# A four-part residual block on one core: the diagonal mix moved within its period, an epsilon added on another engine, and eight weight sums placed in other slots

## Chip, core and metric

One core of a Trainium2 chip runs the whole program. The metric is the time of one execution in device microseconds, the median of several runs. Engines are named as in the profile: PE (TensorE) with PEld for its weight loads, DVE (VectorE), ACT (ScalarE), POOL (GpSimd), SP (SyncE, which here only starts transfers). "L435" is line 435 of the kernel before.

## What is computed

`x` is 64 x 32 x 512 in float32. Four blocks follow each other, each adding its result to `x`; cut to what matters here:

```python
def block0(x, condition, weights):            # W is 32x32 for each of 64 samples
    return einsum('bct,bcd->bdt', x, weights[condition])

def block1(x, adapter_ids, base_weight, base_bias, A_w, B_w):
    result = einsum('bsd,od->bso', x, base_weight) + base_bias
    h = einsum('bsd,brd->bsr', x, A_w[adapter_ids])       # rank 16
    return result + einsum('bsr,bor->bso', h, B_w[adapter_ids])

def block2(x, Wq, Wk, Wv, Wo, q_norm_w, k_norm_w, k_cache, v_cache, table, seqlens):
    q, k, v = heads(x @ Wq.T), heads(x @ Wk.T), heads(x @ Wv.T)   # 32 / 8 / 8 heads of 128
    q, k = rope(rmsnorm(q, q_norm_w)), rope(rmsnorm(k, k_norm_w))
    # rmsnorm: t * rsqrt(mean(t*t) + EPS) * w
    keys, values = paged_cache(k_cache, table) + k, paged_cache(v_cache, table) + v  # 512 + 32
    probs = softmax(where(valid, q @ keys.T / sqrt(128), -1e30))
    return (probs @ values) @ Wo.T

x = x + block0(...); x = x + block1(...); x = x + block2(...)
x = x + block3(...)                            # as block0, other weights
```

The change touches block 0 (the mix), the rmsnorm of block 2, and the preparation of block 2's projection weights.

## The kernel before

**Tiles.** The 2048 rows of `x` form 16 tiles of 128 rows, each holding four samples. Block 0 is one matmul for a tile: four 32 x 32 matrices are spread into a 128 x 128 block-diagonal matrix (`diagonal`, L426: the gathered rows `mix_rows` times a mask `same`), multiplied with the tile (`mix`, L435), and added to it on DVE (`add`, L444). Block 1 needs the tile transposed (`turn_x`, L452), the low-rank product `h` (`ranks`, L474), its mask (`own_ranks`, L484, DVE), and a linear product in five chunks (`linear`, L490): four of the base weight, the fifth with the masked ranks `hT`. GpSimd adds the bias (L447). The result is turned again (`turn_out`) and stored for block 2. Tiles are taken in pairs; each second tile also makes sums and differences of the pair's transposed halves (`sums`, L516 to 520), because the projections are done with seven products instead of eight, from sums of inputs and sums of weights.

**Projections.** Eight key heads are done in two groups of four. In each group, eight pairs of tiles are projected; a pair has three blocks of seven products each: keys and values, and two for the queries. `project` (L651) issues two matmuls for each product into `proj_ps`, which is one PSUM bank, and `take` (L663, DVE; ACT for the first of a block) adds it to what was kept. Products 1, 4, 5, 6 of a queries' block, and two of the keys' and values' block, start a `Norm`: `squares` (L707, four ACT instructions with a running sum), `power` (L712 adds epsilon on DVE, L714 raises to the power -1/2 on GpSimd), and then four pieces `scale`, `straight`, `swapped`, `sum` on DVE, and a turn on PE. `swapped` and `straight` read the rotary tiles `rot_q` and `rot_k`, which SP loads for each pair (`load_rotary`, L591).

**Weight sums.** `block_sum` (L615, DVE, 1.14 us each) makes the sums of weights for a group: four for keys and values (`KV`), four each for query blocks 0 and 1. The query sums are made in the first pair's window of a group.

**Attention.** 512 units of work, one for each sample and key head, follow each other: scores against 544 keys (L838, L841), a masked maximum and softmax (L846, L857, L863), a transposition of the weights (L880, L882), and the product with the values (L893), whose rows GpSimd gathers (`v_sb`, L105). GpSimd also makes the penalty mask of a sample (`pen`, L809), 2.23 us each. The last phase, from about 2112 us, multiplies with `Wo` and adds block 3.

**Order.** Every engine works its queue in the order in which the program was written, and that is set by a hand-made plan: time is cut into slots, an attention slot lasting about 3.66 us. `at(slot, where, ...)` puts a step into a list of a slot, and `slot(i)` issues the lists one after the other:

```python
run(i, "fetch"); run(i, "pool")      # transfers
...                                   # scores of this unit, flip of an earlier one
run(i, "pe"); run(i, "late"); run(i, "power")
norm_piece(i)
... ; run(i, "turn") ; ...            # values, divide
run(i, "dve")
norm_piece(i); norm_piece(i)
run(i, "keep"); run(i, "act"); run(i, "store")
```

Norm pieces wait in a queue of their own, and a slot takes one only while its count `busy[slot]` is under 2 (3 in every fourth slot); a `block_sum` puts 2 on the count of its slot.

The slots before attention form the prologue (0 to about 240 us). There a tile `t` has a home slot -39 + 2t, so that a period is two slots. In the first slot of the period of tile t, PE does the mix of t, projections of an earlier pair, the ranks and linear chunks 0 to 2 of t-1, and the turn of t-2. In the second it does linear chunks 3 and 4 of t-1, projections, and the turn of t. On DVE the first slot has `own_ranks` of t-1 and the add of the mix of t, ahead of its "dve" list (takes, `block_sum`); the second has the add of the linear result of t-1 and then its "dve" list: `sums`, the diagonal of t+1, rotary tiles (L382), takes. The cache's key pages are turned as well, four of them in the first slots (class `Turn`).

Of the kernel before, what the change touches and what calls it, by code (L numbers as in the profile page):

```python
# [30 lines left out]
ALU = mybir.AluOpType  # L31
# [17 lines left out]
D = 128  # L49
# [10 lines left out]
EPS = 1e-6  # L60
# [17 lines left out]
def resid_kernel(  # L78
# [19 lines left out]
    nc = tc.nc  # L98
# [129 lines left out]
    with ExitStack() as l2:  # L228
# [468 lines left out]
        class Norm:  # L697
# [11 lines left out]
                    )  # L709

            def power(self):
                nc.vector.tensor_scalar(self.ss, self.ss, D * EPS, None, ALU.add)  # L712
                self.rstd = small.tile([P, REP], F32, name="rstd")
                nc.gpsimd.tensor_tensor(  # L714
                    self.rstd, self.ss, minus_half.to_broadcast([P, REP]), ALU.pow
                )
# [220 lines left out]
        def at(slot, where, do, *args):  # L937
            plan.setdefault((slot, where), []).append((do, args))
# [56 lines left out]
        def make(table, key, what, *args, **kw):  # L995
            table[key] = what(*args, **kw)
# [5 lines left out]
        for i in range(n_pairs):  # L1002
            home = WINDOW * (i - 1) - AHEAD
            g, p = divmod(i, NT // 2)
            if i == 0:
                at(home - 10, "fetch", make, pair_of, 0, Pair, 0)
            for w, name in ((23, "a"), (26, "12"), (29, "34"), (30, "b")):
                if i + 1 < n_pairs:
                    if name == "a":
                        at(home + w, "store", make, pair_of, i + 1, Pair, i + 1)  # L1010
                    at(home + w, "store", call, pair_of, i + 1, "load", name)
            if i == 0:
                at(home + 4, "store", call, pair_of, 0, "load", "b")
            if i:
                at(home + 2, "fetch", call, pair_of, i, "load_rotary", "k")
                at(home + 9, "fetch", call, pair_of, i, "load_rotary", "q")
            for b, slots in (
                (KV, (0, 0, 1, 2, 3, 3, 4, 5, 6, 6, 7, 8, 9, 9)),
                (0, (10, 11, 12, 12, 13, 14, 15, 15, 16, 17, 18, 18, 19, 20)),
                (1, (21, 21, 22, 23, 24, 24, 25, 26, 27, 27, 28, 29, 30, 30)),  # L1020
            ):
                slots = [home + w for w in slots]
                at(slots[0], "fetch", begin_block, i, b, slots)
            if p == 0:
                sums = [(b, what) for b in (0, 1) for what in (3, 2, 1)] + [(0, 4), (1, 4)]
                for w, one in zip((5, 6, 7, 9, 10, 11, 17, 18), sums):
                    at(home + w, "dve", block_sum, *one)
                    busy[home + w] = busy.get(home + w, 0) + 2
                for w, what in zip((-1, 0, 2, 5) if g == 0 else (-19, -16, -13, -10), (3, 2, 1, 4)):
                    at(home + w, "dve", block_sum, KV, what)  # L1030
                    busy[home + w] = busy.get(home + w, 0) + 2
            if p == NT // 2 - 1:

                if g == NG - 1:
                    loads = [(load_o_weights, k) for k in range(2 * KG)]
                else:
                    loads = [(load_kv_weights, g + 1, k) for k in (1, 0)]
                    loads += [(load_q_weights, g + 1, k) for k in range(KG)]
                if g == NG - 1:
                    places = (  # L1040
                        (7, 8), (11, 12), (16, 18), (20, 21), (23, 25), (36, 38), (27, 29), (24, 26)
                    )
                else:
                    places = ((3, 4), (9, 10), (14, 15), (21, 22), (25, 26), (32, 33))
                for slots, load in zip(places, loads):
                    for j, w in enumerate(slots):
                        at(home + w, "store", *load, j, nc.gpsimd)
# [4 lines left out]
        for t in range(NT):  # L1052
            home = -WINDOW - AHEAD - 6 + 2 * t
            f = [first_of, t]
            at(home - 5 if t > 1 else begin, "fetch", make, *f, First, t)
            at(home - 4 if t > 1 else begin, "fetch", call, *f, "load")
            at(max(begin, home - 4) if t > 1 else begin, "pool", call, *f, "fetch")
            if t % 2 == 0:
                at(home - 3 if t else begin, "pool", call, *f, "fetch_a")
            at(home - 2, "dve", call, *f, "diagonal")  # L1060
            at(home - 1, "pe", call, *f, "mix")
            at(home - 1, "power", call, *f, "add")
            if t % 2 == 0:
                at(home, "turn", call, *f, "turn_a")
                at(home, "keep", call, *f, "keep_a")
            at(home, "turn", call, *f, "turn_x")
            at(home, "keep", call, *f, "keep_x")
            at(home + 1, "pool", call, *f, "bias")
            at(home + 1, "late", call, *f, "ranks")
            at(home + 1, "power", call, *f, "own_ranks")  # L1070
            at(home + 1, "late", call, *f, "linear", (0, 1, 2))
            at(home + 2, "pe", call, *f, "linear", (3, 4))
            at(home + 2, "power", call, *f, "add")
            at(home + 3, "store", call, *f, "store_x")
            at(home + 3, "turn", call, *f, "turn_out")
            at(home + 3, "keep", call, *f, "keep_out")
            at(home + 4, "store", call, *f, "store")
            if t % 2:
                at(home + 4, "dve", call, *f, "sums")
                at(home + 5, "store", call, *f, "store_sums")  # L1080

            home = SLOTS * t + 9
            turning.add(home)
            at(home - 6, "fetch", lambda t: make(turn_of, t, Turn, 1, t, room["pages"], 1), t)
            at(home, "turn", call, turn_of, t, "turn")
            at(home, "keep", call, turn_of, t, "keep")
            at(home + 1, "store", call, turn_of, t, "store")
        for c in range(NT):


            home = -27 + c if c > 3 else begin + 3 + c
            key = -1 - c
            at(home - 3 if c > 3 else begin, "fetch", make, turn_of, key, Turn, 0, c, start_pool, 5)
            where = "turn" if c > 3 else "pe"
            at(home, where, call, turn_of, key, "turn")
            if 0 < c < 4:
                plan[home, where].insert(0, plan[home, where].pop())
            at(home, "keep", call, turn_of, key, "keep")
            at(home + 1, "store", call, turn_of, key, "store")
            home = -27 + max(c - 1, 0) * 10 // NT  # L1100
            at(home, "dve", rotary, c)
            at(home, "store", store_rotary, c)
# [54 lines left out]
        home = n - 33  # L1157
# [132 lines left out]
    with ExitStack() as l3:  # L1290
        sums = l3.enter_context(tc.tile_pool(name="sums", bufs=1))
# [196 lines left out]
```

## Time and profile before

| | us |
|---|---|
| median of three runs | 2515.36 |
| the three runs | 2513.62, 2515.36, 2519.85 |
| the profiled execution | 2515.45 |
| its span | 2513.7 |
| PE busy | 2454.2 (13760 instructions) |
| DVE busy | 1626.6 (3762) |
| ACT busy | 1398.6 (4135) |
| POOL busy | 1124.8 (936) |

The span is what the profile divides; some 1.7 us of the execution lie around it. A row of a group of instructions gives line, engine, operation, output and inputs, the number of instructions, their busy time and mean duration, and how long the engine was idle just ahead of them and for whom. A row of the waits reads "engine, what it was about to do, whom it waited for: total us, times, longest". A row of the timeline has start and duration in us; consecutive instructions of one kind are one row with a count, and the bracket at the end is the idle time before it and its releaser. A releaser ending in "q" or an engine ending in "q" is the engine's queue of transfers.

### The profile page before, as it was taken

To read this page: it belongs to the slowest core of one execution; us is meant where nothing else is said; L and a number is where in the kernel's file an instruction comes from. 1 tells how busy PE (TensorE), PEld (TensorE's weight loads), DVE (VectorE), ACT (ScalarE), POOL (GpSimd) and SP (SyncE) were. 2 spreads that over 40 slices of the span, in tenths; PEclk is the share of its full clock that TensorE was granted. 3 is DMA by queue.
4 is the path that set the end of the run, shared out by engine and by line. 5 is a ranking of instruction groups with operands and counts; after the bars stand their busy time and mean duration, and the time that the engine had idled before them with its cause. 6 is when DMAs were issued, how large, how long until landed. Compare 5 with 4: busy or idle time off the path is not lost.

```text
span 2513.7 us, 47403 instructions
## 1 busy us (share of the span) xinstructions
PE 2454.2 (98%) x13760; PEld 1863.4 (74%) x13760; DVE 1626.6 (65%) x3762; ACT 1398.6 (56%) x4135; POOL 1124.8 (45%) x936
## 2 busy tenths in 40 slices
PE   6888999999999999999999999999999999999999
PEld 3445777777777777767777777777777788888887
DVE  5656777777777677767776777777777766433222
ACT  2124777777777676757676777777677765000000
POOL 4334555555555555645455555555555663000000
PEclk9999999999999999999999999999999999999999
DMA  7675666666666667756565656565657784333221
GB/s 234 220 236 168 186 198 188 197 194 197 183 203 184 197 192 246 238 179 187 176 186 172 202 173 190 176 187 177 186 173 222 248 257 149 126 124 127 86 84 60
DMA packets 448546, 459.19 MB, mean 183 GB/s; under 512 B 51424, under 2 KB 379488, under 8 KB 440480
## 3 DMA queue, kind: packets, MB, share of 16 engines
q1 hardware_dynamic: 398384, 291.24, 37.4%
q0 software_dynamic: 49904, 164.93, 21.8%
q8 instruction: 112, 1.84, 0.3%
q14 instruction: 146, 1.20, 0.2%
HBM read 384.66 MB, written 79.69 MB: 185 GB/s over the span
## 4 chain that ended last, share of the span: by engine, by line
PE 92%; DVE 2%; DMA 2%; issue 2%; SPq 1%; POOL 0%; ACT 0%; DVEq 0%; ACTq 0%
PE proj_ps L651 22%; PE o_ps L893 17%; PE out_ps L1312 15%; PE s_ps L838 10%; PE s_ps L841 8%; PE pT_ps L880 8%; PE head_ps L756 3%; PE l_ps L490 2%; PE o_ps L905 2%; DMA kT<-kT 1%; SPq L794 1%; PE h_ps L474 1%; PE mix_ps L435 1%; PE s_ps L873 1%; PE mix_ps L1330 1%
## 5 line engine op out<-in xcount | busy, mean ns | idle before, releaser
L105 POOL DMA_INDIRECT v_sb<-v,v_rows x512 | 525.1, 1026 | 359.6 <-PE o_ps L893 248.3
L846 DVE CUSTOM_DVE_ANT_0 sm<-s_ps,pen 128x544 f32<-128x544 f32 x512 | 370.6, 724 | 462.8 <-PE s_ps L841 445.9
L893 PEld LDWEIGHTS o_ps<-pT,v_sb 128*128 128x128 f32 x4096 | 519.8, 192 | 133.1 <-issue 125.0
L857 ACT ACTIVATE sm<-sm,top 128x544 f32<-128x544 f32 x512 | 382.0, 746 | 344.1 <-DVE top L846 343.7
L893 PE MATMUL o_ps<-pT,v_sb 128*128 128x128 f32 x4096 | 541.7, 275 | 1.5 <-DMA v_sb<-v,v_rows 1.5
L863 ACT ACTIVATE sm<-sm,share 128x512 f32<-128x512 f32 x512 | 369.9, 722 | 174.6 <-DVE share L862 169.0
L714 POOL TENSOR_TENSOR rstd<-ss,minus_half 128x4 f32<-128x4 f32 x160 | 208.1, 1301 | 527.5 <-DVE ss L712 527.4
L882 DVE COPY pT<-pT_ps 128x512 f32<-128x512 f32 x512 | 350.9, 685 | 1.9 <-PE pT_ps L880 1.9
L838 PE MATMUL s_ps<-kT,qT 128*128 128x288 f32 x1024 | 347.6, 421 | 3.5 <-DMA kT<-kT 3.3
L841 PE MATMUL s_ps<-kT,qT 128*128 128x256 f32 x1024 | 305.6, 380 | 3.7 <-DMA kT<-kT 3.7
L880 PE MATMUL pT_ps<-ident,sm 128*128 128x128 f32 x2048 | 308.0, 273 | 0.0
L880 PEld LDWEIGHTS pT_ps<-ident,sm 128*128 128x128 f32 x2048 | 256.3, 141 | 51.6 <-issue 0.2
L809 POOL TENSOR_SCALAR pen<-key_f,seq_f 128x544 f32<-128x544 f32 x128 | 285.5, 2231 | 10.8
L841 PEld LDWEIGHTS s_ps<-kT,qT 128*128 128x128 f32 x1024 | 194.6, 190 | 59.2 <-issue 4.3
L663 DVE TENSOR_TENSOR raw<-proj_ps,raw 128x512 f32<-128x512 f32 x332 | 223.1, 684 | 10.2 <-PE proj_ps L651 4.7
L707 ACT ACTIVATE sq<-raw 128x128 f32<-128x128 f32 x640 | 197.1, 308 | 33.3 <-DVE raw L663 18.1
L651 PE MATMUL proj_ps<-sum,x 128*128 128x512 f32 x380 | 189.6, 602 | 2.7 <-DVE raw L663 2.6
L1362 ACT COPY p<-out_ps 128x256 f32<-128x256 f32 x7 | 2.6, 372 | 333.1 <-PE out_ps L1312 298.1
L105 POOL DMA_INDIRECT mix_rows<-in_w,cond_rows x32 | 33.1, 1034 | 312.9 <-DVE mix_diag L171 300.0
L838 PEld LDWEIGHTS s_ps<-kT,qT 128*128 128x128 f32 x1024 | 155.1, 191 | 20.3 <-issue 4.0
L1312 PE MATMUL out_ps<-w,o_in 128*128 128x256 f32 x768 | 167.1, 379 | 0.0
L1312 PEld LDWEIGHTS out_ps<-w,o_in 128*128 128x128 f32 x768 | 145.9, 190 | 19.8
(175 smaller groups left out, 3391.1 us busy)
## 6 DMA issues: line engine op xcount, KB each, us to landing
kT<-kT SPq DMA_DIRECT2D x2048, 64.0 KB
o<-oT SPq DMA_DIRECT2D x29, 1024.0 KB
o_in<-o SPq DMA_DIRECT2D x28, 1024.0 KB
page_rows<-in_kv_cache SPq DMA_DIRECT2D x32, 256.0 KB
v<-in_kv_cache SPq DMA_DIRECT2D x32, 256.0 KB
kT<-page_rows SPq DMA_DIRECT2D x32, 256.0 KB
vn<-raw SPq DMA_DIRECT2D x32, 256.0 KB
v_sb<-v,v_rows POOLq DMA_INDIRECT x512, 4.1
```

Of the source, the lines that this page charges most:

```text
L105: nc.gpsimd.indirect_dma_start(out=dst, out_offset=None, in_=table, in_offset=bass.IndirectOffsetOnAxis(ap=index, axis=0),)
L651: nc.tensor.matmul(self.ps, lhsT=self.pair.x[x][:, c if x == "b" else half.start + c, :], rhs=blocks(self.b)[w][:, c, :], start=(c == 0), ...
L809: nc.gpsimd.tensor_scalar(self.pen, key_f, seq_f[:, self.b : self.b + 1], BIG, ALU.is_ge, ALU.mult)
L838: nc.tensor.matmul(ps[:, first:HID], lhsT=q, rhs=self.kT[:, :n1, k, :], start=True, stop=True)
L841: nc.tensor.matmul(ps[:, HID : first + LA], lhsT=q, rhs=self.kT[:, n1:, k, :], start=True, stop=True)
L846: nc.vector.tensor_tensor_reduce(out=sm, in0=ps[:, first : first + LA], in1=self.pen, scale=1.0, scalar=3e38, op0=ALU.add, op1=ALU.min, ac ...
L857: nc.scalar.activation(sm, sm, AF.Exp, bias=top, scale=-1.0, accum_out=total)
L863: nc.scalar.activation(sm[:, :L], sm[:, :L], AF.Copy, scale=share)
L880: nc.tensor.transpose(ps[:, c, :], self.sm[k][:, c * P : (c + 1) * P], ident)
L882: nc.vector.tensor_copy(pT, ps)
L893: nc.tensor.matmul(self.o_ps[k], lhsT=self.v[c][:, k * D : (k + 1) * D], rhs=self.pT[k][:, c, :], start=(c == 0), stop=False,)
L1312: nc.tensor.matmul(ps[:, :HALF], lhsT=o[:, i, :], rhs=w[i // REP][:, i % REP, :], start=(i == 0), stop=(i == KG * REP - 1),)
```

## The change

Three edits, all to the plan or to the engine that an operation runs on.

1. The diagonal of a tile is made in the list "power" of its slot instead of "dve", that is directly after the add of the linear result; the mix is issued from the list "late" instead of "pe", that is after the ranks and linear chunks 0 to 2 of the tile before. The first page's turn goes to "late" with it.
2. The epsilon in `Norm.power` is added by GpSimd instead of DVE.
3. The eight query sums of a group's first pair go to other slots, in another order: from offsets 5, 6, 7, 9, 10, 11, 17, 18 to 5, 7, 10, 13, 15, 17, 20, 23.

```diff
             def power(self):
-                nc.vector.tensor_scalar(self.ss, self.ss, D * EPS, None, ALU.add)
+                nc.gpsimd.tensor_scalar(self.ss, self.ss, D * EPS, None, ALU.add)
                 self.rstd = small.tile([P, REP], F32, name="rstd")
                 nc.gpsimd.tensor_tensor(
                     self.rstd, self.ss, minus_half.to_broadcast([P, REP]), ALU.pow
                 )
...
             if p == 0:
-                sums = [(b, what) for b in (0, 1) for what in (3, 2, 1)] + [(0, 4), (1, 4)]
-                for w, one in zip((5, 6, 7, 9, 10, 11, 17, 18), sums):
-                    at(home + w, "dve", block_sum, *one)
+                for w, b, what in (
+                    (5, 0, 3),
+                    (7, 0, 2),
+                    (10, 0, 1),
+                    (13, 1, 3),
+                    (15, 1, 2),
+                    (17, 0, 4),
+                    (20, 1, 1),
+                    (23, 1, 4),
+                ):
+                    at(home + w, "dve", block_sum, b, what)
                     busy[home + w] = busy.get(home + w, 0) + 2
...
-            at(home - 2, "dve", call, *f, "diagonal")
-            at(home - 1, "pe", call, *f, "mix")
+            at(home - 2, "power", call, *f, "diagonal")
+            at(home - 1, "late", call, *f, "mix")
             at(home - 1, "power", call, *f, "add")
...
-            where = "turn" if c > 3 else "pe"
+            where = "turn" if c > 3 else "pe" if c else "late"
             at(home, where, call, turn_of, key, "turn")
```

No instruction is added or removed in all: 160 of them go from DVE to GpSimd, and the rest change places. The order in which SP starts its transfers is the same.

## The prediction

> **What bounds the kernel now.** I read the page first: busy shares, the slices, the shares of the chain.
>
> ```profile
> PE 2454.2 (98%) x13760; PEld 1863.4 (74%) x13760; DVE 1626.6 (65%) x3762; ACT 1398.6 (56%) x4135; POOL 1124.8 (45%) x936
> ...
> PE   6888999999999999999999999999999999999999
> ...
> PE 92%; DVE 2%; DMA 2%; issue 2%; SPq 1%; POOL 0%; ACT 0%; DVEq 0%; ACTq 0%
> ```
>
> TensorE is busy nearly everywhere and carries 92% of the chain. Its count of matmuls stays, so the change can win only where PE idles or is clocked down: the first four slices of 63 us. The second view is busy time by stretch (PE, PEld, DVE, ACT, POOL, then the granted clock, DMA share, GB/s).
>
> ```profile
> 28.10:57.10 29.00, 24.61 (x83) 13.61 (x84) 21.84 (x39) 5.66 (x8) 10.18 (x8) 0.88 0.58 189
> 57.10:98.00 40.90, 34.23 (x122) 18.31 (x121) 23.69 (x54) 7.64 (x18) 12.74 (x11) 0.96 0.65 209
> 98.00:139.00 41.00, 33.41 (x119) 18.11 (x118) 26.29 (x70) 9.66 (x28) 13.15 (x10) 0.92 0.76 242
> 139.00:180.00 41.00, 35.77 (x150) 21.26 (x148) 23.11 (x47) 12.48 (x34) 15.59 (x13) 0.96 0.78 240
> 180.00:211.00 31.00, 30.09 (x110) 16.56 (x111) 16.28 (x32) 8.48 (x26) 8.52 (x10) 0.94 0.39 126
> 211.00:241.00 30.00, 23.37 (x84) 13.59 (x83) 22.37 (x52) 17.14 (x50) 18.19 (x17) 0.89 0.68 208
> 300.00:900.00 600.00, 600.00 (x3603) 452.13 (x3602) 431.26 (x1055) 429.57 (x1288) 316.80 (x251) 1.00 0.66 195
> 1104.00:1118.00 14.00, 10.65 (x44) 7.57 (x43) 5.51 (x13) 5.99 (x18) 4.46 (x5) 0.76 0.64 181
> ```
>
> In steady attention PE has 600 of 600 us. In the prologue's periods (28 to 211) it idles 4.39+6.67+7.59+5.23+0.91 = 24.8 us, at the hand-over to attention (211 to 241) 6.6, at the switch between groups of heads (1104 to 1118) 3.35. Third, who is waited for, and one prologue period on the timeline:
>
> ```profile
> PE mix_ps L435 <- DVE mix_diag L426: 28.8, 11, 8.8
> PE proj_ps L651 <- DVE raw L663: 11.9, 7, 5.3
> ...
> POOL rstd L714 <- DVE ss L712: 527.4, 158, 8.9
> ```
>
> ```profile
> 97.75 0.60 PE L452 MATMUL x1T_ps<-ident,x_sb 128*128 128x128 f32 x4
> 100.64 1.13 PE L435 MATMUL mix_ps<-x_sb,mix_diag 128*128 128x512 f32 x2 [2.29 <-DVE mix_diag L426]
> ```
>
> Within 28 to 211 the diagonal costs PE 20.0 us over ten waits, the one proj bank 5.4 over three. In the period shown PE stands 2.29 us at the mix because DVE makes the diagonal (at 100.31) only after four L516-520 sums.
>
> [...] after 5.28 us of idling for `raw` at 222.96, four passes of projections took 3.78 us, where two at 216.65 took 1.02; after 4.16 us of idling at 49.02 the mix took 2.07 us instead of the 1.13 below. [...] at 98.56 one L519 sum took 1.49 us beside a bias add, its neighbours 0.41 to 0.42. [...] The pow of 1.40 us at 337.14 is followed by a gather at 338.73: 1.6 us by starts, so the rows serve.
>
> **Part 1: mix to the period's end, diagonal to its front.** Per tile PE's order was: mix, projections, ranks h, linear 0-2 | linear 3-4, projections, turns; the bar separates the two slots. Now the mix stands before the bar. One matmul (two passes, 0.86 us) moves behind h (0.89) and linear 0-2 (2.58), so it ends about 3.4 us later relative to them; the first page turn (four transposes, 0.44) moves in the same slot. The diagonal (one DVE operation, 0.28) moves ahead of sums, rotary and take. SP's order and the gathers of mix_rows on POOL stay. No instruction is added.
> Removed: the 20.0 us of waits at L435 in the periods. The other 8.8 are the program's first wait, for a gather of mix_rows that lands at 8.49; they stay.
> Added: DVE's add L444 keeps its place (hT, add, then its list) and now waits for the late mix. Queued behind it are the sums, rotary tiles and L663 takes, and the next projection waits for the take, since proj has one bank. Worked for one period with the sums (tiles at slots -26/-25): after the mix, hop 0.27, add 0.60, list 1.14+1.62; then add-linear and diagonal 0.80; then sums 1.46, rotary 0.81, take 1.20, and 1.07 for the collision with the bias add; hop back 0.13. From its second slot on that makes 9.1 us against 3.5 of PE work: 5.6 us of stall. By the same sum the periods come to 1.6, 2.3, 0, 4.1, 5.6, 1.6, 4.4, 2.9, 0, 0.6, 3.3, 0, 0.4 = 26.8 us, against 24.8 + 1.6 (one mix at the edge) = 26.4 before. Clock: (1-PEclk) times length was 11.9 us; I estimate 10.6 from the new stall lengths. So the large wait is replaced by the bank's wait, nearly even: **-1 us**, bounds -10 (DVE slips under the matmuls oftener than I sum) and +10 [...].
>
> **Part 2: epsilon on GpSimd.** 160 operations of L712 (0.16 us each, 26 us) leave DVE; POOL gets 160. In steady state PE has no idle time, so DVE's 26 us are worth nothing; they hid under 600/600 us of PE. POOL's eps now waits for ACT's squares, and behind it stand the pow L714 (1.30), penalty masks (2.23) and v_sb gathers. POOL reaches pow already waiting (527.4 us at L712), so the wait changes owner. The price of a 128x4 constant add on POOL isn't shown. Bounds 0.1 (the 128x1 memset is 0.09) and 1.3 (pow, same shape); I take 0.35 with the semaphore hop to pow. Cover: the gather at 338.73 lands after a median 4.1 us, needed at 345.46: 2.6 us of margin, so 0.35 and even 1.3 stay hidden. If that cover goes, o_ps waits for v_sb. Cost 0, bounds 0 and +5.
> At the hand-over it does count: DVE stood for ACT's squares before L712 (1.85+1.25+1.25 us) with takes behind it, and PE waited 5.28 us for one. Afterwards the kT loads, issued when PE's last scores bank is free near 211 and landed at 226.45, come next. Gain **-2**, bounds -4 and 0.
>
> **Part 3: the sums of queries' weights.** Eight L615 operations (1.14 us, no DMA) per group go from offsets 5-18 to 5-23. Each blocks norm pieces in its slot, so the pieces move too; total work is the same. In the first group this is in the hand-over. At the switch it decides a queue:
>
> ```profile
> SPq L591 <- DVE share L862: 9.1, 1, 9.1
> ```
>
> ```profile
> 1089.16 9.85 SPq L591 DMA_DIRECT2D rot_q<-rot  x2
> 1099.82 9.43 SPq L794 DMA_DIRECT2D kT<-kT  x16
> ...
> 1110.39 1.30 PE L838 MATMUL s_ps<-kT,qT 128*128 128x288 f32 x2 [3.35 <-DMA kT<-kT]
> ```
>
> SP waits 9.1 us until the last norm of the old pair has read rot_q, 16 kT loads are queued behind, and PE stands 3.35 us. With the sums spread that last reader comes four slots earlier (229 instead of 233, load in 232; a slot is 3.66 us): the loads start some 9 us sooner. Gain 3.35 + slow clock (14 us at 0.76, less the idle: 2.95) = **-6.3**, bounds -6.3 and -3 (take waits instead).
>
> **Sum.** -1 -2 -6.3 = -9.3. The profiled execution took 2515.45 (span 2513.7 and 1.7 around it), the median is 2515.36: **2506**.
>
> **Rivals.** *A, as summed*: 2506 +- 5. Chance 0.44; of it 0.31 falls under 2507.8. I count 0.3%, 7.5 us, as what a measurement of this kernel can tell from no change.
> *B, prologue gains too*: for it speaks that DVE is busy only 24 to 26 of 41 us in a period, and that the ten diagonal stalls were also what let the clock drop. -8 to -13 more: 2493 to 2498, say 2496. Chance 0.22.
> *C, switch or prologue gives it back*: at the switch another load of the same SP queue comes last (-3), or the prologue loses 6: 2511 to 2515. Against: `kT` alone ended PE's wait there. Chance 0.20.
> *D, slower: the late mix holds up DVE.* DVE waits up to 3.4 us for the mix in each of 12 periods, 41 us, against 26.4 us of idling now: +15 if nothing covers it, and stalls of 4 to 6 us drop the clock, 2 to 9 us more: prologue +17 to +24, less 8.3 from elsewhere = +9 to +16, or 2524 to 2531. It decides once the prologue loses over 15.8 us (7.5 + 8.3). For it speaks that the proj bank already ends waits of 5.3 us; against, that DVE has 40% of the period free. Chance 0.14, with it POOL's gathers late through eps costing over 2.6 us.
> **Numbers.** Faster 0.31 + 0.22, with 0.01 of C: 0.54. Same 0.13 of A and 0.18 of C: 0.31. Slower D's 0.14 and 0.01 of C: 0.15. Range 2493 to 2521: it leaves out D's upper half and B's tail.
>
> **What would show it.** Right: the wait of mix_ps on mix_diag gone; proj_ps on raw (PE and PEld) up from 11.9 us to some 25 or 30; x_sb L444 waiting for mix_ps; PE idle in 28 to 211 near 26 us; no 9.1 us wait at L591 and no kT stall near 1100; L712 on POOL, 160 of 0.1 to 0.4 us, the rstd wait turned into one for ACT's sq; o_ps still waiting only 1.5 us for v_sb. Wrong: PE idle in 28 to 211 under 18 or over 36 us; a kT stall at the switch that stays; v_sb waits in hundreds of places.

## The result and the profile after

The changed kernel takes **2499.06 us** (median of 7 runs, 2497.4 to 2502.9) against 2515.53 us before (7 runs, 2510.53 to 2519.85). The ratio is 0.9936, interval 0.9923 to 0.9949: 16.1 us faster (12.8 to 19.4). The forecast was 2506 us, range 2493 to 2521. The profiled execution took 2498.24 us, its span is 2496.5.

The page of the kernel after, the rows that answer to those shown of before: busy times, PE in 40 slices, shares of the chain, and the group of the moved epsilon.

```profile
PE 2445.1 (98%) x13760; PEld 1857.8 (74%) x13760; DVE 1609.0 (64%) x3602; ACT 1398.9 (56%) x4135; POOL 1163.0 (47%) x1096
...
PE   7799999999999999999999999999999999999999
...
PE 92%; DMA 2%; DVE 2%; issue 2%; SPq 1%; POOL 1%; ACT 0%; DVEq 0%; POOLq 0%; ACTq 0%
...
L712 POOL TENSOR_SCALAR ss<-ss 128x4 f32<-128x4 f32 x160 | 54.1, 338 | 448.0 <-ACT sq L707 447.6
```

PE does the same 13760 matmuls but is busy 9.1 us less: at half clock the same matmuls take longer (four passes of L651 took 3.78 us at a granted clock of 0.50 in before, and 1.98 at 1.00 in after), so less half-rate time shows as less busy time (worked out for the periods below). 160 instructions went from DVE to POOL, each 0.34 us on the mean (0.238 at the median).

The waits of the kernel after (who waited, at what, for whom: total us, times, longest):

```profile
POOL ss L712 <- ACT sq L707: 447.6, 156, 7.3
...
DVE x_sb L444 <- PE mix_ps L435: 37.9, 13, 4.1
...
PE proj_ps L651 <- DVE raw L663: 17.1, 10, 4.1
...
PE mix_ps L435 <- DVE mix_diag L426: 7.3, 1, 7.3
```

PE's wait for the diagonal is gone but for the first, at the program's start. In its place DVE waits for the mix (37.9 us) and PE for takes: 17.1 us under that name, and 5.08 us more that the trace calls "issue". The timeline shows that this, too, is a take; DVE first, then PE:

```profile
85.51 0.69 DVE L444 TENSOR_TENSOR x_sb<-mix_ps,x_sb 128x512 f32<-128x512 f32 x1 [3.14 <-PE mix_ps L435]
86.12 1.22 DVE L615 TENSOR_TENSOR sum<-wq,wq 128x1024 f32<-128x1024 f32 x1
...
89.47 0.96 DVE L426 TENSOR_TENSOR mix_diag<-mix_rows,same 128x128 f32<-128x128 f32 x1
...
92.62 1.28 DVE L663 TENSOR_TENSOR raw<-proj_ps,raw 128x512 f32<-128x512 f32 x2
```

```profile
94.00 3.65 PE L651 MATMUL proj_ps<-sum,x_b 128*128 128x512 f32 x4 [5.08 <-issue]
```

DVE stood 3.14 us for the late mix, went through its list, and finished both takes of that product at 93.90; PE's next projection, which needs the one bank, starts at 94.00.

I divide the span at events that all kernels have: the first turn of tile 2 (x1T) starts the periods, the last turn of tile 15 (x2T) ends them; the hand-over then runs to the first product with values of unit 29; around the group switch I take the stretch from the products of unit 231 to those with the new values (L905) of units 256 to 259. (Where an expectation names units 32 and 288, it counts nine products to a unit; there are ten.) Busy time by stretch for these three stages, of before and after (columns: PE, PEld, DVE, ACT, POOL, granted clock, DMA share, GB/s):

```profile
35.18:213.20 178.02, 153.29 (x560) 84.94 (x559) 108.22 (x237) 43.93 (x114) 59.02 (x52) 0.93 0.65 206
213.20:347.90 134.70, 128.07 (x715) 92.87 (x713) 96.60 (x234) 93.56 (x284) 75.79 (x61) 0.97 0.65 191
1101.40:1215.07 113.67, 109.34 (x639) 81.70 (x637) 82.66 (x195) 76.53 (x229) 55.69 (x44) 0.97 0.64 189
```

```profile
35.31:207.51 172.20, 149.84 (x560) 82.52 (x559) 105.17 (x229) 44.24 (x114) 59.35 (x59) 0.95 0.67 213
207.51:338.43 130.92, 125.63 (x715) 91.36 (x714) 95.26 (x223) 93.65 (x284) 79.13 (x74) 1.00 0.66 196
1093.08:1198.67 105.59, 105.59 (x635) 79.26 (x633) 82.09 (x185) 76.03 (x228) 59.67 (x53) 1.00 0.65 195
```

Length less PE busy is PE's idle time. Beside it stands, under "clock", the most that half-rate stretches (granted clock 0.50) can cost: half their length, from the clock's record in the trace, which is finer than the rounded column. PE may idle in part of such a stretch, and then it costs less. All in us:

| kernel | periods: length (idle, clock) | hand-over | switch |
|---|---|---|---|
| before | 178.0 (24.7, 11.9) | 134.7 (6.6, 3.4) | 113.7 (4.3, 3.4) |
| after | 172.2 (22.4, 8.5) | 130.9 (5.3, 0) | 105.6 (0, 0) |
| e1 diagonal early, mix late | 172.4 (24.0, 8.5) | 135.1 (7.1, 3.4) | 112.8 (4.6, 1.7) |
| e2 epsilon on GpSimd | 174.9 (24.8, 8.5) | 131.2 (5.6, 0) | 112.6 (4.4, 1.7) |
| e3 sums spread | 171.6 (22.8, 6.8) | 137.9 (8.8, 3.4) | 105.7 (0.1, 0) |
| e4 diagonal early alone | 160.4 (14.9, 5.1) | 134.8 (7.5, 1.7) | 112.5 (4.1, 1.7) |
| e5 mix late alone | 175.8 (25.2, 10.2) | 134.9 (6.9, 3.4) | 111.2 (4.7, 0) |
| e6 after, mix first | 161.5 (13.1, 8.5) | 131.2 (4.4, 1.7) | 105.6 (0, 0) |
| e7 rot_q loaded later | 175.3 (24.8, 8.5) | 135.0 (6.9, 3.4) | 107.2 (1.0, 0) |
| e10 mix first, takes early | 145.5 (4.9, 0) | 130.9 (3.2, 1.7) | 105.6 (0, 0) |
| e11 after, epsilon on DVE | 172.8 (23.7, 8.5) | 135.2 (6.6, 3.4) | 105.7 (0.1, 0) |
| e12 before, once more | 175.5 (24.7, 8.5) | 135.3 (7.1, 3.4) | 113.4 (3.9, 3.4) |
| e13 after, once more | 172.5 (22.4, 10.2) | 130.7 (4.9, 0) | 105.6 (0, 0) |
| e14 mix late, takes early | 149.5 (6.9, 1.7) | 131.4 (5.6, 0) | 105.6 (0, 0) |

In the two traces of after against the two of before, means: periods 172.4 against 176.8 (-4.4), hand-over 130.8 against 135.0 (-4.2), switch 105.6 against 113.55 (-8.0). That is 16.6 us. The spans of these traces differ by 15.2 us and the medians of all runs by 16.1, so the three stages are all of the gain; the stretch between hand-over and switch is 1.4 us longer in after. A part of that is only where the mark lies: with the sums spread, four turns of a head (L756, some 0.5 us) come ahead of unit 231's product that came behind it before. In steady attention (300 to 900 us), 600 of 600 us of PE are busy before and after.

In the periods the clock's real cost can be worked out: PE's busy time inside half-rate stretches, halved, is 11.1 and 8.5 us in the two traces of before, 7.7 and 8.0 in those of after. Taken off PE's busy time it leaves 142.2 us in each of the four, so the same work is left once the clock is taken off. Of the 4.4 us, then, 2.4 are idle time and 2.0 are clock, and before alone moves by more than that 2.0 between its own two traces.

### The profile page after: what moved, and what is told of

Its sections match the earlier page's. It is cut to its first block, busy times and chain, and to the rows that moved or that the text cites. A ratio compares the mean times of both kernels' runs of the same rounds, so it can differ in the third digit from the quotient of the medians.

```text
span 2496.5 us, 47363 instructions
## 1 busy us (share of the span) xinstructions
PE 2445.1 (98%) x13760; PEld 1857.8 (74%) x13760; DVE 1609.0 (64%) x3602; ACT 1398.9 (56%) x4135; POOL 1163.0 (47%) x1096
## 3 DMA queue, kind: packets, MB, share of 16 engines
q0 software_dynamic: 49904, 164.93, 21.6%
## 4 chain that ended last, share of the span: by engine, by line
PE 92%; DMA 2%; DVE 2%; issue 2%; SPq 1%; POOL 1%; ACT 0%; DVEq 0%; POOLq 0%; ACTq 0%
PE proj_ps L651 22%; PE o_ps L893 17%; PE out_ps L1320 15%; PE s_ps L838 10%; PE s_ps L841 8%; PE pT_ps L880 8%; PE head_ps L756 3%; PE l_ps L490 2%; PE o_ps L905 2%; DMA kT<-kT 1%; DMA v_sb<-v,v_rows 1%; SPq L794 1%; PE s_ps L873 1%; PE h_ps L474 1%; PE mix_ps L1338 1%
## 5 line engine op out<-in xcount | busy, mean ns | idle before, releaser
L105 POOL DMA_INDIRECT v_sb<-v,v_rows x512 | 539.2, 1053 | 362.3 <-PE o_ps L893 252.9
L809 POOL TENSOR_SCALAR pen<-key_f,seq_f 128x544 f32<-128x544 f32 x128 | 279.3, 2182 | 11.8 <-DMA kT<-kT 0.5
L712 POOL TENSOR_SCALAR ss<-ss 128x4 f32<-128x4 f32 x160 | 54.1, 338 | 448.0 <-ACT sq L707 447.6
L663 DVE TENSOR_TENSOR raw<-proj_ps,raw 128x512 f32<-128x512 f32 x332 | 223.5, 685 | 9.7 <-PE proj_ps L651 4.4
L707 ACT ACTIVATE sq<-raw 128x128 f32<-128x128 f32 x640 | 197.1, 308 | 29.7 <-DVE raw L663 14.5
L651 PE MATMUL proj_ps<-sum,x 128*128 128x512 f32 x380 | 189.7, 602 | 8.0 <-DVE raw L663 7.9
L714 POOL TENSOR_TENSOR rstd<-ss,minus_half 128x4 f32<-128x4 f32 x160 | 183.0, 1144 | 13.3
```

The lines of the kernel that those rows point to most:

```text
L105: nc.gpsimd.indirect_dma_start(out=dst, out_offset=None, in_=table, in_offset=bass.IndirectOffsetOnAxis(ap=index, axis=0),)
L651: nc.tensor.matmul(self.ps, lhsT=self.pair.x[x][:, c if x == "b" else half.start + c, :], rhs=blocks(self.b)[w][:, c, :], start=(c == 0), ...
L809: nc.gpsimd.tensor_scalar(self.pen, key_f, seq_f[:, self.b : self.b + 1], BIG, ALU.is_ge, ALU.mult)
```

## Experiments

"Before" stands for the runs of the kernel before beside each; gains are worked out as (1 - ratio) times its median.

**e1: diagonal early and mix late, alone.** The third and fourth hunk of the diff.

```diff
-            at(home - 2, "dve", call, *f, "diagonal")
-            at(home - 1, "pe", call, *f, "mix")
+            at(home - 2, "power", call, *f, "diagonal")
+            at(home - 1, "late", call, *f, "mix")
...
-            where = "turn" if c > 3 else "pe"
+            where = "turn" if c > 3 else "pe" if c else "late"
```

> Part 1 alone (diagonal early, mix late, first page turn with it); epsilon on DVE and the sums' slots as before. Theory: each part acts in a stage of its own. The prologue's last turn of a tile (x2T of tile 15; 213.2 us before, 207.5 after) comes at 207 to 209, the hand-over and the group switch stay as before (9.1 us wait of SP at L591, 3.35 us kT stall near the switch), so 5 to 6 us faster than before: 2509 to 2511. Rival: the prologue gained because DVE no longer stops for ACT's squares at L712 (8.5 us of such waits before); then the last turn stays near 213 and the time within 2 us of before.

Measured: 2512.54 us, ratio 0.9987 (0.9979 to 0.9995), 3.3 us faster. The last turn came at 206.8, just ahead of what the theory had, but idle time in the periods fell only by 0.7 us; the rest of that trace's shorter prologue was the clock (8.5 us at most, for 11.9 before) and a start 0.8 us sooner, and the time gained is under the 5 to 6 expected. Part 1 is a little gain, not the main one. The rival's cause, an epsilon taken off DVE, is absent here; e2 looks at it alone.

**e2: epsilon on GpSimd, alone.**

```diff
-                nc.vector.tensor_scalar(self.ss, self.ss, D * EPS, None, ALU.add)
+                nc.gpsimd.tensor_scalar(self.ss, self.ss, D * EPS, None, ALU.add)
```

> Part 2 alone (epsilon on GpSimd). Theory: no gain in steady attention (PE has no idle time there); prologue unchanged within 2 us; hand-over 2 to 4 us shorter (from the last turn of a tile to the first product with values 25.4 us before, 22.0 after), since DVE no longer waits for squares ahead of the take that held PE for 5.28 us. 2 to 4 us faster: 2511 to 2513. Rival: the sums' slots shortened the hand-over and epsilon does nothing: 25 us there, time as before within 1.5 us. Second rival: DVE's 26 us matter all over: 10 us or more.

Measured: 2511.7 us, ratio 0.998 (0.9971 to 0.999), 5.0 us faster. Periods unchanged in idle time (24.8), which also answers the rival of e1; hand-over 131.2 us, 3.5 to 4.1 shorter than in the two traces of before. The mechanism holds; the gain lies above the 2 to 4 us expected, though its interval (2.5 to 7.3) reaches into them.

**e3: sums spread, alone.** The list of eight slots of the diff.

```diff
-                for w, one in zip((5, 6, 7, 9, 10, 11, 17, 18), sums):
-                    at(home + w, "dve", block_sum, *one)
+                for w, b, what in ((5, 0, 3), (7, 0, 2), (10, 0, 1), (13, 1, 3), ...
+                    at(home + w, "dve", block_sum, b, what)
```

> Part 3 alone (query sums in other slots). Theory: the wait of SP at L591 of 9.1 us falls under 1 us, no kT stall at the switch, and no half-rate stretch there: the stretch around the switch is 7 to 8 us shorter; prologue unchanged; hand-over within 2 us. 6 to 9 us faster: 2506 to 2509. Rival: the switch only clears if pieces also run sooner because DVE has no epsilon; then the SP wait stays over 4 us and the gain is under 3.

Measured: 2504.13 us, ratio 0.9954 (0.994 to 0.9967), 11.6 us faster. The switch is 8.0 us shorter. SP's wait for the old pair's reader fell from 9.1 us to this, in its waits around the switch:

```profile
SPq L591 <- DVE rot_b L738: 0.2, 1, 0.2
```

The cause at the switch is as expected, and the rival is out: DVE kept its epsilon. The gain is above the 6 to 9 us expected (interval 8.3 to 15.1), and the expectation was wrong in two places: the periods gained 1.9 us of idle time, and the hand-over lost some 2 (8.8 against 6.6 and 7.1).

**e6: the kernel after with the mix back in front.** The diagonal stays early.

```diff
-            at(home - 1, "late", call, *f, "mix")
+            at(home - 1, "pe", call, *f, "mix")
...
-            where = "turn" if c > 3 else "pe" if c else "late"
+            where = "turn" if c > 3 else "pe"
```

> The kernel after with the mix (and the first page turn) put back to the front of its period; the diagonal stays early. Theory: the diagonal's early place alone removes the wait of PE for it, and the late mix only makes DVE wait (37.9 us at L444 for the mix), so putting the mix back is as good or better: 2493 to 2500, prologue's last turn at 202 to 208. Rival: the late mix gives DVE's diagonal the time it needs; with the mix first PE waits for mix_diag again, over 8 us in all, the last turn comes at 210 or later and the time is 2502 to 2506.

Measured: 2488.32 us, ratio 0.9891 (0.9875 to 0.9907), some 11 us under the kernel after and better than expected. Of PE's waits for the diagonal, 20.0 us in ten places before, little comes back between 28 and 211 us:

```profile
PE mix_ps L435 <- DVE mix_diag L426: 3.3, 3, 1.6
```

**The late mix gives back most of what the early diagonal gains.**

**e4 and e5: the two halves of part 1.** e4 has the diagonal's line alone, e5 the other two.

> Only the diagonal's early place; mix first, epsilon on DVE, sums in the old slots. Theory: this edit alone carries the prologue's gain, and moving the mix costs some of it: PE idles some 14 to 17 us between the turns of tiles 2 and 15 (26.3 before, about 20 with the mix late as well), the last turn comes at 199 to 205, 8 to 14 us faster than before. Rival: without the late mix PE stands for the diagonal again, idle over 22 us, and the gain is under 4 us.

> Only the late mix (and the first page turn with it); the diagonal is made where it was, after the sums. Theory: the late mix hides the diagonal by itself but delays DVE as in the kernel after: idle 20 to 25 us between the turns of tiles 2 and 15, 0 to 6 us faster than before, and no slower than the diagonal and the late mix together by more than 3 us. Rival: diagonal and late mix are only worth something together: PE waits for mix_diag over 10 us in all and the time is that of before or worse.

Measured: e4 2502.15 us, ratio 0.9947 (0.9932 to 0.9962), 13.3 us faster; idle in the periods 14.9, the last turn at 196.3, sooner than expected. e5 2517.56 us, ratio 1.000 (0.999 to 1.0011); idle 25.2. Stretch of the periods, e4 then e5:

```profile
35.82:196.25 160.43, 145.55 (x561) 81.42 (x560) 107.94 (x237) 43.94 (x114) 60.17 (x52) 0.97 0.73 229
```

```profile
35.57:211.34 175.77, 150.52 (x560) 83.80 (x559) 108.88 (x238) 44.24 (x114) 60.88 (x52) 0.94 0.65 209
```

The waits of PE in 28 to 211 us of e5 say what the late mix does without an early diagonal: it removes the wait for mix_diag and puts these in its place.

```profile
PE proj_ps L651 <- DVE raw L663: 17.6, 8, 4.4
PE proj_ps L651 <- issue: 5.6, 1, 5.6
```

The "issue" is a take once more: DVE's two L663 end at 98.74, PE's matmuls start at 98.84. With 2.7 us of waits for ACT this makes 17.6 + 5.6 + 2.7 = 25.9 us, against 20.0 + 5.4 + 0.9 = 26.3 before: an even exchange. So the theory of e5 holds in its mechanism, with no gain and with idle just above the 20 to 25 us; its rival is right on the time but not on the cause, for the wait for mix_diag is gone. (The 26.3 us of e4's expectation are counted from 28 us on; from the turn of tile 2 they are 24.7.)

**e7: SP's load of rot_q three slots later, nothing else.**

```diff
-                at(home + 9, "fetch", call, pair_of, i, "load_rotary", "q")
+                at(home + 12, "fetch", call, pair_of, i, "load_rotary", "q")
```

> The kernel before with one number changed: SP's load of rot_q is issued three slots later in every pair (offset 12 instead of 9); the sums stay packed. It leaves the old pair's last reader where it was and takes only SP's wait for it. Theory: that wait, with 16 kT loads behind it, was the whole cost at the group switch: the wait at L591 falls under 1 us, PE has no kT stall there, from unit 288's place to the next mark the stretch is 7 to 8 us shorter, as with the spread sums. Rival: the packed sums also hold DVE's takes there, PE waits for raw instead, and over 3 us of the stall stay.

Measured: 2511.78 us, ratio 0.9981 (0.9971 to 0.9991), 4.8 us faster. The switch took 107.2 us, 6.3 under the mean of the two traces of before, with no kT stall and an L591 wait of

```profile
SPq L591 <- DVE sum L615: 0.4, 1, 0.4
```

so the queue behind SP's wait was the cause of that stall. What is left of idle there (1.0 us) is takes, which the spread sums also remove; with it the stretch falls just short of the 7 to 8 us expected. In this trace 1.97 us of waiting for v_sb at 987 us took some of the gain back; whether the moved load caused that wait was not tried.

**e11: the kernel after with the epsilon on DVE.** The line of e2, reversed, in the kernel after.

> The kernel after with the epsilon back on DVE (late mix, early diagonal and spread sums stay). In the trace of the spread sums alone the hand-over was longer, not shorter (137.9 us from the last turn to unit 32's product, against 134.7 before and 131.2 with epsilon alone). Theory: spread sums put norms next to the last takes, so that DVE's stop for ACT's squares costs more; here the hand-over is 136 to 139 us and the kernel 4 to 8 us slower than after: 2503 to 2507. Rival: the two do not meet, hand-over 131 to 134 us, 2498 to 2502.

Measured: 2503.13 us, ratio 0.9961 (0.9947 to 0.9974). That is 4 us slower than after by the medians and 6 by the two ratios to before, as expected; hand-over 135.2, just short of what was expected, and no longer than before's 134.7 and 135.3, so the lengthening that the theory starts from, seen in e3, is not seen here. The waits of PE in 205 to 245 us of this kernel, and of the kernel after:

```profile
PE proj_ps L651 <- DVE raw L663: 3.4, 1, 3.4
...
PE head_ps L756 <- DVE rot_a L748: 1.5, 1, 1.5
```

```profile
PE s_ps L838 <- DMA kT<-kT: 2.4, 1, 2.4
PE proj_ps L651 <- DVE raw L663: 1.7, 1, 1.7
```

Idle in the hand-over differs by only 1.3 us (6.6 and 5.3); the rest is half-rate time, 3.4 at most: the granted clock is 0.97 over the hand-over of e11 and 1.00 over that of after, whose longest stall there is 2.4 us.

**e12 and e13: both kernels, once more.**

> The kernel before, unchanged, looked at once more. Theory: PE's idle time in the prologue repeats (24.7 us between the turns of tiles 2 and 15, within 0.5), while what the half-rate windows cost there (11.9 us in the first trace) does not[...]: 5 to 12 us, and the stage is longer or shorter by just that. Rival: the half-rate windows stand at the same instructions again, 11.9 us.

> The kernel after, unchanged, looked at once more. Theory: idle in the prologue 22.4 us within 0.5, half-rate windows costing something other than 8.5 us there, between 5 and 14; no half-rate window at the group switch. Rival: 8.5 us again, at the same instructions.

One execution each, 2511.5 and 2498.28 us. Idle in the periods repeats to the tenth (24.7; 22.4). The half-rate stretches do not: the bound is 8.5 where it was 11.9, and 10.2 where it was 8.5. Before's periods were 2.5 us shorter in the second trace for no change of program. After's were 0.3 longer only, since PE stood still in more of the half-rate time: the clock's real cost is 7.7 and 8.0 us. Outside the periods idle time repeats less well: 0.4 to 0.5 us apart in the hand-over and at before's switch.

**e10: mix first and the takes ahead of the lists.** The answer to the stalls that are left in e6.

```diff
-                at(last, "act" if i == 0 else "dve", block.take, i, norm)
+                at(last, "act" if i == 0 else "take" if last < -3 else "dve", block.take, i, norm)
...
             run(i, "power")
+            run(i, "take")
```

> The kernel after with the mix put back to the front, and in the prologue the takes (L663) issued on DVE right after the adds and the diagonal, ahead of sums, rotary tiles and weight sums. Theory: what stalls are left in the prologue come from takes behind those lists (one proj bank): idle between the turns of tiles 2 and 15 falls from 14.5 us (mix first) to under 5, the half-rate stretches with it; 2474 to 2484. Rival: DVE's total work bounds these periods, the stall moves to x2T or the sums' stores; then idle stays over 10 us and the time within 4 us of 2488.

Measured: **2474.95 us**, ratio 0.9835 (0.9818 to 0.9852), 41.5 us faster than before. Idle in the periods 4.9 us (the table has 13.1 for e6, where the expectation has 14.5), no half-rate stretch:

```profile
36.03:181.54 145.51, 140.64 (x561) 79.32 (x559) 106.88 (x227) 43.62 (x114) 62.66 (x59) 1.00 0.79 252
```

DVE's busy time there is what it was (106.9 against 106.3 in e6): its load did not bound the periods, the place of the take in its queue did.

**e14: mix late, takes early.** The edit of e10 in the kernel after.

> The kernel after (mix late) with the prologue's takes issued on DVE right after the adds and the diagonal, ahead of sums, rotary tiles and weight sums. Theory: the late mix does harm only through the list that stands behind DVE's wait for it, ahead of the takes; with the takes in front its cost is mostly gone: idle between the turns of tiles 2 and 15 falls from 22.4 to 4 to 9 us (4.9 with the mix first), 2474 to 2482. Rival: the late mix itself (a chain from mix over add to the turn of the next slot) costs PE some 10 us as it did beside the early diagonal: idle 13 to 16 us, 2484 to 2490.

Measured: 2475.23 us, ratio 0.9852 (0.9826 to 0.9877); idle 6.9. The theory holds: against after only the takes' place differs, and 21 us are gone by the ratios to before, 24 by the medians. With the takes in front, the mix's place is worth some 2 us of idle time, and the two kernels' times can't be told apart.

## Why the prediction was right, and where its sum was short

**Direction, range, order of the parts: right.** All three stages named gained, the switch most, steady attention nothing; tried alone, the parts gain in the order forecast (3.3, 5.0, 11.6; the intervals of the first two overlap). The forecast of 9.3 us was short of 16.1.

**Part 1, -1 us: the mechanism and nearly the size.** The step "the large wait is replaced by the bank's wait, nearly even" is what happened. The stalls summed slot by slot stand in the trace of after in their places: 5.6 forecast for the period with the sums and 5.08 found, 4.4 and 4.09, 2.9 and 2.77, 3.3 and 3.16. Together 26.8 were forecast and 21.6 found. More than half of the surplus lies in the tiles at -32 and -28 (2.3 and 4.1 forecast, 1.06 and 2.49 found); the price of running beside the bias add was too high where it can be seen: 0.68 us (mix_diag at 89.47, beside the bias add at 89.02, 0.96 instead of 0.28) for 1.07. Of the signs named, the wait for takes came to 17.1 + 5.1 = 22.2 us, under the 25 to 30 forecast, and PE's idle time in 28 to 211 to 22.6 for 26. Alone, part 1 gained 3.3 us (1.3 to 5.3). What the prediction did not see is that the part is made of two edits that cancel: the early diagonal alone is worth 13.3 us, and the late mix, worth nothing alone (e5), costs some 10 of it. Rival D, DVE held up by the late mix, was true as a mechanism and nearly in its price (37.9 us of DVE waiting for 41); it just did not exceed what the diagonal freed.

**Part 2, -2: the mechanism right, the term too small.** e2 gained 5.0 us, and the hand-over of after is 4.2 us shorter, both past the bound of -4. The step that failed is pricing the 5.28 us stall by its idle time only. Idle in the hand-over fell by some 1.8 us, near the 2 forecast, with the wait for kT coming next as the prediction had it (2.4 us, above); but the granted clock is also 0.50 from 221.98 to 228.80, 6.83 us, which cost up to 3.4. The stall before, and what is left of it in after:

```profile
222.96 3.78 PE L651 MATMUL proj_ps<-wv,x_a 128*128 128x512 f32 x4 [5.28 <-DVE raw L663]
```

```profile
213.66 1.98 PE L651 MATMUL proj_ps<-wv,x_a 128*128 128x512 f32 x4 [1.67 <-DVE raw L663]
```

The four passes take 3.78 us at a granted clock of 0.50 and 1.98 at 1.00. All eight traces with the epsilon on DVE have half-rate time in the hand-over (seven of them 3.4, one 1.7); of the six with it on GpSimd four have none and two 1.7. On POOL the operation took 0.34 us on the mean (0.35 was taken), 0.78 at most, and o_ps waited 2.4 us for v_sb in all, 1.5 before: the cover held.

**Part 3, -6.3: right at the switch, wrong in the first group.** Cause and queue are as predicted (e7 shows it by itself). The size was 8.0: idle was 3.9 to 4.3 us where 3.35 was taken, since takes of the packed sums held PE for 0.8 us more at 1138, the half-rate stretch (granted clock 0.50 from 1109.44 to 1116.27) lasted 6.83 us and cost at most 3.4 where 2.95 was taken, and some 0.5 are the four turns that only crossed the mark. The sentence "in the first group this is in the hand-over" is wrong: with the first pair's home in slot -33, the eight sums stand in slots -28 to -10, amid the periods. There the spread cuts a stall of 2.83 us to 0.63, and e3's idle falls by 1.9; I worked with the new places in the stalls but gave the part no gain of its own for it. Whether the spread costs something in the hand-over stays open: e3, with the epsilon on DVE, has 8.8 us of idle there, 3.0 of them for v_sb, but e11, which also has the sums spread and the epsilon on DVE, has 6.6, as before.

**The terms side by side**: forecast -1, -2, -6.3; found in the traces -4.4, -4.2, -8.0. The stages are not quite the parts: of the idle time gone from the periods (2.4 us), e1 shows 0.7 for part 1 and e3 1.9 for part 3. Of the 7.3 us between the sums, 3.4 are the periods, where the rest of the gain is half-rate time, which moved the stage by 0.3 and 2.5 us between two executions of one program; that share is luck as much as forecast. So the time lies nearer to rival B's 2496 than to A's 2506, though hardly for B's reason: half-rate time did go with the diagonal's stalls, but it went with the stalls that replaced them nearly as much (at most 11.9 and 8.5 us in the periods of before, 8.5 and 10.2 in those of after).

The single effects 3.3, 5.0 and 11.6 add to 19.9 us against 16.1 together; their intervals (some 2 us each way for the first two, 3 for the third) cover that, and I do not read an interaction out of it.

The prediction priced stalls of 2.3 us by their length alone. The one ahead of 74.74 in before was followed by half-rate time that cost 1.7 us more (last section).

## What to carry to other kernels

When two edits to one queue travel together, try each alone: an early diagonal worth 13 us was delivered with a late mix that gave 10 back. If PE waits on a single PSUM bank, try the read-out that frees it ahead of whatever in DVE's list nobody waits for yet: here that was worth 13 us and more with the mix first and over 20 with the mix late, while DVE stayed as busy as before. Price a PE stall by its length and by what the clock adds (up to 3.4 us here beside the stall of 5.28 us), and compare idle time stage by stage before comparing times, which carry the luck of the clock: in the periods idle time repeated to the tenth.

## What was not expected of the hardware

A stall of 2.29 us came with half-rate time in one trace and without it in another. In before, behind the stall of 2.29 us ahead of 74.74, the granted clock was 0.50 from 75.20 to 78.62, with PE busy throughout, which cost 1.7 us. In e2 the same stall, of the same length, cost nothing, and the stretch from the turn of tile 5 to that of tile 6 took 12.49 us in place of 14.17. What decides between the two is not shown. The mix behind that stall, before and in e2:

```profile
74.74 1.65 PE L435 MATMUL mix_ps<-x_sb,mix_diag 128*128 128x512 f32 x2 [2.29 <-DVE mix_diag L426]
```

```profile
75.23 1.12 PE L435 MATMUL mix_ps<-x_sb,mix_diag 128*128 128x512 f32 x2 [2.29 <-DVE mix_diag L426]
```

Between two executions of one program the clock made 2.5 us in the periods of before and 0.3 in those of after. It is not all of the scatter of 9 us among the runs of before: from the end of the switch stretch to the last phase its two traces took 914.1 and 911.0 us, and over the fourteen this stretch lies between 911.0 and 920.4, with 3.4 to 9.1 us of idle time, in part for kT between 2000 and 2080 us, and with half-rate time, in the first trace of before from 2034.45 to 2037.87, which cost at most 1.7 us. Why those waits differ was not tried, and a gain of a few us is safer read from the stage it belongs to than from a whole execution.
